# A fifth tile of rows by one-hot matmuls in 15 of 196 chunks, and moved zeros, of a graph-network kernel

## The chip, the cores and the metric

The kernel runs on one core of a Trainium2 chip. The metric is the time of one execution on the device in microseconds (us); lower is better. The core has a tensor engine (TensorE, PE in the profile, with its weight loads as PEld), a vector engine (DVE), a scalar engine (ACT), GpSimd (POOL) and a sync engine (SP). They run their own instruction streams and meet through semaphores. DMA transfers are issued by SP and ACT (queues "SPq" and "ACTq" in the profile) and by POOL, which issues the indirect ones.

## The reference

One layer of a graph network on 12,500 nodes with 32 features and 400,000 edges that are sorted by their target node:

```python
h = jnp.maximum(_layernorm(x, axis=-1), 0.0)
rol, col = (src, dst)
e_feat = jnp.concatenate([h[rol], h[col], edge_attr], axis=-1)
hid = jax.nn.relu(e_feat @ W1 + b1)                 # 96 -> 64
v = hid @ W2 + b2                                   # 64 -> 32
x_cand = jax.ops.segment_max(v, col, num_segments=num_nodes)
out = x + jnp.maximum(x_cand, h)
```

## The kernel before

**Tiling.** The nodes are padded to 12,544 = 128 x 98. The edges are cut into four stripes (NS = 4), which lie side by side on the 128 partitions, 32 features each. A chunk is 512 edges of each stripe, so 2,048 edges; there are 196 chunks. The main loop (from L530) takes two chunks c and c + 1 in an iteration, 98 iterations in all, and prepares chunks a = c + 2 and b = c + 3 for the next.

**Source rows.** For the 2,048 edges of a chunk the rows h[src] are wanted, 16 groups ("tiles") of 128. They come in two ways:

- Twelve by gathers: `gather(c)` (L148) issues twelve indirect DMAs on POOL, one for 128 rows of `h_d` in device memory. Three gathers share a buffer `gh`, and there are 24 buffers, so POOL can run ahead of their use by six chunks and then waits until DVE has read a buffer.
- Four by matmuls (MM = 4), in all chunks but the last: `tile(c, m)` (L227). The table h stands in `hs` as two parts, grouped by 7 (A1) groups of 14 (A0) nodes per partition. A key says which partition and group a source node lies in. `one_hots` (L202, DVE, five of the seven groups) and `one_hots_act` (L210, ACT, the other two) compare the keys with each partition's number and give `hot`. Seven times two matmuls of 448 columns in `tile` pick out, for each edge, the 14 nodes of its group; DVE multiplies them by a mask (`one`, L242) and reduces them (`gm`, L243) to the row. The products lie in two rotating PSUM buffers `pv`, which also hold the result of the second layer.

`to_features` (L245) transposes the rows to features on partitions, into `ht`: three gathered tiles at a time (L256), then the four from the matmuls (L259). L256 is what frees a `gh` buffer.

**Layers.** PE sums three products for each stripe into `ph`: edge attributes (`edges_into`), windows of the target nodes' part (`windows_into`) and `ht` (L548). ACT applies relu (`hid`, L552). PE multiplies by W2 (L569). DVE runs a segmented maximum along the edges (`sm`, L576). `leave_1` transposes it back (L473) and adds the bias (L475); `leave_2` selects the last edge of each node (L483, L487) and stores windows of 32 nodes into one of two tables, `top_d` (L491).

**Order.** Under `manual_schedule` the order of SP, PE, DVE and ACT is as written. In an iteration PE has tile(a, 0), the `ht` products of chunk c, tile(a, 1), tile(a, 2), the edge products of a, the W2 products, the window products of a, `leave_2` of the chunk before, tile(a, 3), `leave_1(c)`, tile(b, 0), `leave_2(c)`, tile(b, 1), `leave_1(c + 1)`, tile(b, 2) and tile(b, 3). POOL has little but gathers.

**Ahead of the loop.** h is computed in four pieces (three on DVE, one summed on POOL, squares on ACT, L327), stored to `h_d` (L337), and the gathers start. Keys are computed (L176 to L178) and stored to `key_d`, then read back repeated over the partitions (`load_keys`, L187). Just ahead of the loop ACT issues two DMAs that fill both tables `top_d` with zeros (L523), because not every node gets a store.

**Behind the loop.** A flag `general_i` says whether the input breaks the assumption that 512 edges of a stripe reach fewer than 32 nodes; it is computed by DVE and PE inside iteration 182 (L603 to L611). All engines load it and branch (L621, L622); with this input the general path is not taken. Then SP reads `top_d[0]` (L698) and ACT `top_d[1]` (L699), and DVE takes the maximum of both (L702), of that and h (L703), adds x (L704), and SP stores the output (L705), in four pieces.

Of the kernel before, what the change touches and what calls it, by code (L numbers as in the profile page):

```python
# [8 lines left out]
F32 = mybir.dt.float32  # L9
F32R = mybir.dt.float32r  # L10
F16 = mybir.dt.float16
# [12 lines left out]
P = 128  # L24
N = 12500
E = 400000
D = 32
# [26 lines left out]
LOW = 1e30  # L54
BY_ACT = range(A1 - 2, A1)
# [5 lines left out]
def ap(t, offset, dims):  # L61
    return bass.AP(tensor=t.tensor, offset=t.offset + offset, ap=dims)
# [3 lines left out]
def gnn_kernel(ctx, tc, x, src, src_mm, src_t, dst, dst_ext, lo, lo_c, ends_b, edge_attr, weights, w1, w2, b2, out):  # L66
# [28 lines left out]
    key_d = dram.tile([len(MMC) * MM * P], F16, name="key_d")  # L95
# [25 lines left out]
    for s in range(NS):  # L121
# [5 lines left out]
                   allow_small_or_imprecise_dtypes=True)  # L127
    hs = const.tile([P, 2, A1, D, A0], F32R, name="hs")
# [18 lines left out]

    def gather(c):  # L148
        n = min(K - MM * (c in MMC), (SE - c * C) // D)
        parts = []  # L150
        for k in range(0, n, SOME):
            parts.append(gathered.tile([P, SOME, D], F32, name="gh"))
            for i in range(min(SOME, n - k)):
                nc.gpsimd.indirect_dma_start(  # L154
                    out=parts[-1][:, i, :], out_offset=None, in_=h_d[:, :],
                    in_offset=bass.IndirectOffsetOnAxis(ap=src_i[:, c, k + i:k + i + 1], axis=0))
        return parts
# [13 lines left out]
    hts = {}  # L171
    loaded_b, ats = {}, {}
# [7 lines left out]
    def places(start, stop):  # L180

        se = src_i[:, MMC.start + start:MMC.start + stop, K - MM:]
        pk = place_k.rearrange("p (c m) -> p c m", m=MM)[:, start:stop]
        group(pk, se)
        nc.vector.scalar_tensor_tensor(pk, pk, -float(A0), se, op0=ALU.mult, op1=ALU.add)
# [41 lines left out]
    def tile(c, m):  # L227

        if c not in MMC:
            return  # L230
        if m == 0:
            mm_rows[c] = early.tile([P, MM, D], F32, name="gm", bufs=6)
        hot = hots[c]
        e = slice(m * P, (m + 1) * P)
        po = early_ps.tile([P, C], F32, name="pv", bufs=2)[:, :D * A0]
        for k in range(A1):
            for part in range(2):
                nc.tensor.matmul(po, hot[:, k, e], hs[:, part, k].rearrange("p f a -> p (f a)"),  # L238
                                 start=(k == 0 and part == 0), stop=(k == A1 - 1 and part == 1))
        of_group = po.rearrange("p (f a) -> p f a", a=A0)  # L240
        one = early.tile([P, D, A0], F32, name="one", bufs=2)
        nc.vector.tensor_tensor(one, of_group, masks[c][:, m, None, :].to_broadcast([P, D, A0]), op=ALU.mult)  # L242
        nc.vector.tensor_reduce(mm_rows[c][:, m, :], one, axis=AX.X, op=ALU.max)  # L243

    def to_features(c, part):  # L245

        if c >= NCH:
            return
        if c not in hts:
            hts[c] = early.tile([P, K, D], F32, name="ht", bufs=4)  # L250
        ht = hts[c]
        n = min(K - MM * (c in MMC), (SE - c * C) // D)
        if part < J:
            r = slice(part * SOME, min((part + 1) * SOME, n))
            if r.start < n:
                nc.vector.transpose(ht[:, r].rearrange("p k e -> p (k e)"),  # L256
                                    gh[c][part][:, :r.stop - r.start].rearrange("p k f -> p (k f)"))
        elif c in MMC:
            nc.vector.transpose(ht[:, n:].rearrange("p k e -> p (k e)"),  # L259
                                mm_rows.pop(c).rearrange("p k f -> p (k f)"))  # L260
        elif n < K:
            nc.vector.memset(ht[:, n:], 0.0)
# [26 lines left out]
    with tc.tile_pool(name="nodes", bufs=1) as pool, tc.tile_pool(name="nodes_ps", bufs=2, space=PSUM) as ps:  # L289
        sp = pool.tile([P, len(MMC) * MM], I32, name="sp")  # L290
        nc.scalar.dma_start(sp, src_mm)
        load_block(0, nc.sync)
        zero = early.tile([P, ZERO], F32, name="zero", bufs=1)
# [23 lines left out]
        for k in (0, 1, GP, 2):  # L317
            v, st, r = shares[k]
            n = r.stop - r.start
            total(v, st[:, 0, :n], xs[:, r])  # L320
            mean = st[:, 0, :n, None].to_broadcast([P, n, D])
            if v is nc.vector:
                v.scalar_tensor_tensor(h[:, r], mean, -1.0 / D, xs[:, r], op0=ALU.mult, op1=ALU.add)
            else:
                v.tensor_scalar(st[:, 0, :n], st[:, 0, :n], 1.0 / D, None, op0=ALU.mult)
                v.tensor_tensor(h[:, r], xs[:, r], mean, op=ALU.subtract)
            nc.scalar.activation(sq[:, r], h[:, r], AF.Square)  # L327
        for v, st, r in shares:
            n = r.stop - r.start
            total(v, st[:, 1, :n], sq[:, r])  # L330
            nc.scalar.activation(st[:, 0, :n], st[:, 1, :n], AF.Sqrt, scale=1.0 / D, bias=eps)
# [54 lines left out]
        key = pool.tile([P, len(MMC) * MM], F32, name="key")  # L386
        key16 = pool.tile([P, len(MMC) * MM], F16, name="key16")
# [40 lines left out]
    with tc.tile_pool(name="edges", bufs=3) as pool, tc.tile_pool(name="edges_ps", bufs=1, space=PSUM) as ps:  # L428
# [93 lines left out]
        for t in top_d:  # L522
            nc.scalar.dma_start(ap(t, 0, [[NT * D, P], [ZERO, NT * D // ZERO], [1, ZERO]]),  # L523
                                zero[:, None, :].to_broadcast([P, NT * D // ZERO, ZERO]))
# [5 lines left out]
        for c in range(0, NCH, 2):  # L530
# [10 lines left out]
            if a == NCH - 2:  # L541
                nc.gpsimd.tensor_tensor(again.rearrange("p (g a) f -> p g a f", a=A0),
                                        hs[:, 0].rearrange("p g f a -> p g a f"),
                                        hs[:, 1].rearrange("p g f a -> p g a f"), op=ALU.add)
            tile(a, 0)
# [27 lines left out]
            for x in range(2):  # L573
# [3 lines left out]
                sms.append(sm)  # L577
            tile(a, 3)
            one_hots_act(a + 2)
            to_features(a, 3)  # L580
            to_features(a, J)
# [20 lines left out]
            if c == (NB - 1) * BLOCK:  # L602
                nc.vector.tensor_scalar(bad[:, :NB, 1], bad[:, :NB, 1], float(W), None, op0=ALU.is_ge)  # L603

                nc.vector.tensor_tensor(bad[0:1, NB], lo_i[:, NCH - 1, :2], lo_i[:, 0, 2:], op=ALU.subtract)
                nc.vector.tensor_scalar(bad[0:1, NB], bad[0:1, NB], float(-W), None, op0=ALU.is_gt)
                worst = pool.tile([P, 1], F32, name="worst", bufs=1)
                nc.vector.tensor_reduce(worst, bad, axis=AX.XY, op=ALU.max)
                bp = ps.tile([P, J, P], F32, name="tr")[0:1, 0, 0:1]
                nc.tensor.matmul(bp, worst, ones, start=True, stop=True)  # L610
                nc.vector.tensor_copy(general_i, bp)  # L611
            leave = lambda c=c + 1, so=so, last=last[1]: leave_2(c, so, last)
        leave()


    with tc.tile_pool(name="out", bufs=1) as pool:
        acc = pool.tile([P, NT, D], F32, name="acc")
        part = pool.tile([P, NT, D], F32, name="part")

        top_v = [t.rearrange("(p t) f -> p t f", p=P) for t in top_d]  # L620
        flag = nc.values_load(general_i[0:1, 0:1], min_val=0, max_val=P)  # L621
        with tc.If(flag > 0):  # L622
            with tc.tile_pool(name="general", bufs=1) as gp, tc.tile_pool(name="general_ps", bufs=1, space=PSUM) as ps:
# [69 lines left out]
                nc.vector.memset(part, 0.0)  # L693
                for t, of in zip(top_v, (acc, part)):
                    nc.sync.dma_start(t, of)

        for r in pieces:
            nc.sync.dma_start(acc[:, r], top_v[0][:, r])  # L698
            nc.scalar.dma_start(part[:, r], top_v[1][:, r])  # L699
        out_v = out.rearrange("(p t) f -> p t f", p=P)  # L700
        for r in pieces:
            nc.vector.tensor_tensor(acc[:, r], acc[:, r], part[:, r], op=ALU.max)  # L702
# [66 lines left out]
```

## Time and profile before

| what | us | from |
|---|---|---|
| three runs, median (lowest, highest) | 4136.3 (4134.02, 4138.83) | the runs' times |
| the profiled execution, as given with the runs | 4138.83 | the runs' times |
| its span, first to last instruction | 4137.1 | the profile's page |
| first gather starts | 23.44 | timeline |
| first "hid" of the loop starts | 163.14 | timeline |
| first "hid" of iterations 186, 188, 190 and 192 | 3979.1, 4020.07, 4049.56, 4079.00 | timeline |
| last gather starts | 4014.42 | timeline |
| first read of `top_d` on ACT, on SP | 4113.93, 4115.77 | timeline |
| first maximum of the output, last addition ends | 4122.23, 4134.0 | timeline |

The mean granted TensorE clock of the execution was 0.892.

How to read the profile: a group or timeline row has engine, line, operation, "out<-in" by the program's names, shapes and count ("x14" is fourteen instructions merged into a row). "Idle before" is how long the engine had done nothing ahead of an instruction, with what ended it; "issue" stands for a wait that the profile explains by nothing, "remote" for a semaphore whose setter it does not name. PE's matmuls are pipelined: a row of fourteen lasts less than fourteen times the mean of one. "PEclk" or "clock" is the share of full TensorE clock that was granted, and the DMA share is the mean busy share of the core's 16 DMA engines.

The DMA engines in the first microseconds, from busy time by stage:

| stage, us | 8:10 | 10:12 | 12:14 | 14:16 | 16:18 | 18:20 | 20:22 | 22:24 | 70:75 | 75:80 | 80:85 | 85:90 |
|---|---|---|---|---|---|---|---|---|---|---|---|---|
| DMA share | 0.99 | 0.97 | 0.48 | 0.00 | 0.22 | 0.91 | 0.88 | 0.05 | 0.23 | 1.03 | 0.76 | 0.32 |
| GB/s | 419 | 387 | 165 | 0 | 86 | 362 | 341 | 17 | 64 | 393 | 260 | 67 |

### The profile page before, as it was taken

How to read it: one execution, taken by the hardware profiler on the slowest of the kernel's cores; microseconds unless marked ns; L12 is line 12 of the kernel's file. 1: busy time of each engine (PE TensorE's matmuls, PEld its weight loads, DVE VectorE, ACT ScalarE, POOL GpSimd, SP SyncE). 2: the span in 40 equal slices, each digit the busy share in tenths (PEclk: the TensorE clock that was granted, in tenths of full speed). 3: DMA queues.
4: the chain of work that ended last, by engine and by line, in shares of the span. 5: the costliest groups of instructions: out<-in, count | busy, mean ns of one | idle time of the engine just before them, and what ended most of it. 6: DMA issues, size and time to landing. Idle time of an engine off the chain costs nothing. (4 is left out here: it accounts for less than half of the span.)

```text
span 4137.1 us, 58828 instructions
## 1 busy us (share of the span) xinstructions
PE 3622.7 (88%) x21189; PEld 2423.9 (59%) x21189; DVE 2238.2 (54%) x3869; ACT 1117.3 (27%) x1795; POOL 2258.4 (55%) x2376
## 2 busy tenths in 40 slices
PE   3588888998999998899899999998898889999986
PEld 3456565656566665656565656565656565555664
DVE  4355555555555555555555555555555555555565
ACT  3132223222222222222222232323232323222232
POOL 6555555555555555555555555555555555555550
PEclk7799999989888889999998989898999998988898
DMA  5123222322232222222222222232223222322221
GB/s 196 35 43 64 52 48 43 69 51 44 48 64 53 44 47 65 51 43 52 65 46 46 58 57 49 43 65 53 46 45 66 52 47 46 65 52 44 47 66 51
DMA packets 194678, 229.58 MB, mean 55 GB/s; under 512 B 118333, under 2 KB 158797, under 8 KB 181582
## 3 DMA queue, kind: packets, MB, share of 16 engines
q10 hardware_dynamic: 32580, 110.55, 9.5%
q1 hardware_dynamic: 86762, 76.67, 8.1%
q0 software_dynamic: 75040, 38.57, 7.3%
q8 instruction: 167, 2.74, 0.3%
q14 instruction: 129, 1.06, 0.1%
HBM read 211.68 MB, written 13.85 MB: 55 GB/s over the span
## 5 line engine op out<-in xcount | busy, mean ns | idle before, releaser
L154 POOL DMA_INDIRECT gh<-h_d,src_i x2345 | 2237.3, 954 | 1763.7 <-DVE ht L256 662.3
L238 PE MATMUL pv<-hs,hot 128*128 128x448 f32 x10920 | 2432.0, 373 | 261.3 <-DVE one L242 112.5
L238 PEld LDWEIGHTS pv<-hs,hot 128*128 128x128 f32 x10920 | 2014.1, 190 | 596.2 <-issue 208.3
L242 DVE TENSOR_TENSOR one<-pv,mask 128x448 f32<-128x448 f32 x780 | 480.0, 615 | 1740.3 <-PE pv L238 832.3
L552 ACT ACTIVATE hid<-ph,wt 128x512 f32<-128x512 f32 x392 | 266.2, 688 | 1945.9 <-PE ph L497 632.1
L207 DVE TENSOR_TENSOR hot<-kb,consts 128x1536 fp32r<-128x1536 f16 (+2 forms) x388 | 565.9, 1458 | 0.0
L243 DVE TENSOR_REDUCE gm<-one 128x32 f32<-128x448 f32 x780 | 483.7, 620 | 26.9
L497 PE MATMUL ph<-ea,wt 32*64 32x512 f32 x1568 | 381.8, 781 | 122.3 <-issue 103.1
L569 PE MATMUL pv<-hid,wt 64*32 64x512 f32 x1568 | 341.2, 1008 | 56.8 <-DVE one L242 51.2
L217 ACT ACTIVATE hot<-away,ones 128x512 fp32r<-128x512 f32 x392 | 283.4, 723 | 93.1 <-ACT away L216 52.1
L576 DVE TENSOR_TENSOR_SCAN sm<-pb,sm,pv 128x512 f32<-128x512 bf16 x195 | 249.5, 1280 | 93.5 <-PE pv L569 71.1
L487 ACT ACTIVATE wo<-tr 128x64 f32<-128x64 f32 x196 | 43.8, 223 | 908.0 <-remote 634.4
L216 ACT ACTIVATE away<-kb,key_n 128x512 f32<-128x512 f16 x392 | 277.9, 709 | 0.0
L497 PEld LDWEIGHTS ph<-ea,wt 32*64 32x64 f32 x1568 | 83.2, 149 | 327.6 <-issue 287.0
L483 PEld LDWEIGHTS tr<-so,last 128*64 128x64 f32 x3136 | 126.0, 157 | 184.9 <-issue 155.2
L569 PEld LDWEIGHTS pv<-hid,wt 64*32 64x32 f32 x1568 | 37.3, 133 | 319.1 <-DVE one L242 222.5
L256 DVE STREAM_TRANSPOSE ht<-gh 128x96 f32<-128x96 f32 x782 | 209.8, 268 | 0.0
L497 PE MATMUL ph<-of,qw 32*64 32x512 f32 x1568 | 189.6, 1027 | 0.9 <-issue 0.8
L483 PE MATMUL tr<-so,last 128*64 128x64 f32 x3136 | 155.6, 249 | 8.0 <-issue 4.1
L459 ACT ACTIVATE of<-db,below 128x512 f32<-128x512 int32 x196 | 139.0, 709 | 18.4 <-DMA db<-in_dst_ext 18.4
L460 ACT ACTIVATE of<-of,ones 128x512 f32<-128x512 f32 x196 | 141.5, 722 | 6.4
L497 PE MATMUL ph<-ht,wt 32*64 32x512 f32 x1568 | 126.2, 618 | 8.7 <-DVE ht L259 5.5
(77 smaller groups left out, 783.9 us busy)
## 6 DMA issues: line engine op xcount, KB each, us to landing
ea<-in_edge_attr SPq DMA_DIRECT2D x49, 1024.0 KB
db<-in_dst_ext ACTq DMA_DIRECT2D x48, 1024.0 KB
gh<-h_d,src_i POOLq DMA_INDIRECT x2345
pb<-pen_d ACTq DMA_DIRECT2D x48, 512.0 KB
kb<-key_d ACTq DMA_DIRECT2D x95, 256.0 KB
qw<-q_d SPq DMA_DIRECT2D x784, 8.0 KB
top_d<-wo SPq DMA_DIRECT2D x784, 4.0 KB
top_d<-zero ACTq DMA_DIRECT2D x2, 1568.0 KB
```

The costliest lines, as they stand in the source:

```text
L154: nc.gpsimd.indirect_dma_start(out=parts[-1][:, i, :], out_offset=None, in_=h_d[:, :], in_offset=bass.IndirectOffsetOnAxis(ap=src_i[:, c, ...
L207: nc.vector.tensor_tensor(hot_of(c)[:, start:stop], keys[c][:, None, :].to_broadcast([P, n, MM * P]), key_ps[:, start:stop, None].to_broad ...
L216: nc.scalar.activation(away, keys[c], AF.Square, bias=key_n[:, k:k + 1])
L217: nc.scalar.activation(hot_of(c)[:, k], away, AF.Relu, bias=ones, scale=-1.0)
L238: nc.tensor.matmul(po, hot[:, k, e], hs[:, part, k].rearrange("p f a -> p (f a)"), start=(k == 0 and part == 0), stop=(k == A1 - 1 and par ...
L242: nc.vector.tensor_tensor(one, of_group, masks[c][:, m, None, :].to_broadcast([P, D, A0]), op=ALU.mult)
L243: nc.vector.tensor_reduce(mm_rows[c][:, m, :], one, axis=AX.X, op=ALU.max)
L483: nc.tensor.matmul(pw[g * 2 * W:(g + 1) * 2 * W], last[:, j, 2 * g:2 * g + 2].rearrange("p s w -> p (s w)"), so[:, j, g * 2 * D:(g + 1) * ...
L497: nc.tensor.matmul(ph[s][x * HID:(x + 1) * HID], w[g], e[g], start=start, stop=stop)
L552: nc.scalar.activation(hid[s], ph[s], AF.Relu, bias=b1c)
L569: nc.tensor.matmul(pv[x][s * D:(s + 1) * D], w2x[g], hid[s][g], start=True, stop=True)
L576: nc.vector.tensor_tensor_scan(sm, loaded.pop(c + x)[2], pv[x], before, op0=ALU.add, op1=ALU.max)
```

## The change

1. In chunks 6, 18, 30, ... 174 (MORE, 15 chunks, always an `a` of the loop) only eleven tiles are gathered. The twelfth comes by `tile_more`: a key load of 32 KB on ACT's queue (`load_more`), a one-hot over all seven groups and a mask on DVE (`hot_more`), fourteen matmuls, multiplication, reduction (`pick`, which `tile` now uses too) and a transpose of its own. The one-hots, mask and row have buffers of their own.
2. The zeros of `top_d` are issued in front, on ACT's queue behind the first two squares, instead of just ahead of the loop. Their source buffer goes to the pool that ends with that stage.
3. The flag is computed behind the loop instead of in iteration 182.
4. The tables are read and their maximum is taken ahead of the branch, and the general path overwrites `acc` instead of rewriting the tables.

```diff
+MORE = range(6, NCH - 12, 12)
...
+    def gathers(c):
+        return min(K - MM * (c in MMC) - (c in MORE), (SE - c * C) // D)
+
     def gather(c):
-        n = min(K - MM * (c in MMC), (SE - c * C) // D)
+        n = gathers(c)
...
+        more = src_i[:, MORE.start:MORE.stop:MORE.step, K - MM - 1]
+        for pk, se in ((place_k.rearrange("p (c m) -> p c m", m=MM)[:, start:stop],
+                        src_i[:, MMC.start + start:MMC.start + stop, K - MM:]),
+                       (place_m, more))[:1 + (start == 0)]:
+            group(pk, se)
+            nc.vector.scalar_tensor_tensor(pk, pk, -float(A0), se, op0=ALU.mult, op1=ALU.add)
...
+    def load_more(c):
+        if c in MORE:
+            kb = early.tile([P, P], F16, name="kb_more", bufs=1)
+            nc.scalar.dma_start(kb, ap(key_d, (len(MMC) * MM + MORE.index(c)) * P, [[0, P], [1, P]]))
+            keys_more[c] = kb
+
+    def hot_more(c):
+        if c in MORE:
+            hot = early.tile([P, A1, P], F32R, name="hot_more", bufs=1)
+            nc.vector.tensor_tensor(hot, keys_more[c][:, None, :].to_broadcast([P, A1, P]),
+                                    key_ps[:, :, None].to_broadcast([P, A1, P]), op=ALU.is_equal)
+            mask = early.tile([P, A0], F32, name="mask_more", bufs=1)
+            k = MORE.index(c)
+            nc.vector.tensor_tensor(mask, place_ps, place_m[:, k:k + 1].to_broadcast([P, A0]), op=ALU.is_equal)
+            keys_more[c] = hot, mask
+
+    def tile_more(c):
+
+        if c in MORE:
+            rows = early.tile([P, D], F32, name="gm_more", bufs=1)
+            pick(*keys_more.pop(c), rows)
+            nc.vector.transpose(hts[c][:, K - MM - 1], rows)
...
+            if k < len(top_d):
+                nc.scalar.dma_start(ap(top_d[k], 0, [[NT * D, P], [ZERO, NT * D // ZERO], [1, ZERO]]),
+                                    zero[:, None, :].to_broadcast([P, NT * D // ZERO, ZERO]))
...
-        for t in top_d:
-            nc.scalar.dma_start(ap(t, 0, [[NT * D, P], [ZERO, NT * D // ZERO], [1, ZERO]]),
-                                zero[:, None, :].to_broadcast([P, NT * D // ZERO, ZERO]))
...
+            load_more(a)
             tile(a, 0)
...
+            hot_more(a)
             tile(a, 3)
             one_hots_act(a + 2)
             to_features(a, 3)
+            tile_more(a)
             to_features(a, J)
...
-            if c == (NB - 1) * BLOCK:
-                nc.vector.tensor_scalar(bad[:, :NB, 1], bad[:, :NB, 1], float(W), None, op0=ALU.is_ge)
...
         leave()
+        nc.vector.tensor_scalar(bad[:, :NB, 1], bad[:, :NB, 1], float(W), None, op0=ALU.is_ge)
...
+        for r in pieces:
+            nc.sync.dma_start(acc[:, r], top_v[0][:, r])
+            nc.scalar.dma_start(part[:, r], top_v[1][:, r])
+        for r in pieces:
+            nc.vector.tensor_tensor(acc[:, r], acc[:, r], part[:, r], op=ALU.max)
         flag = nc.values_load(general_i[0:1, 0:1], min_val=0, max_val=P)
...
-                nc.vector.memset(part, 0.0)
-                for t, of in zip(top_v, (acc, part)):
-                    nc.sync.dma_start(t, of)
-        for r in pieces:
-            nc.sync.dma_start(acc[:, r], top_v[0][:, r])
-            nc.scalar.dma_start(part[:, r], top_v[1][:, r])
...
         for r in pieces:
-            nc.vector.tensor_tensor(acc[:, r], acc[:, r], part[:, r], op=ALU.max)
             nc.vector.tensor_tensor(acc[:, r], acc[:, r], again[:, r], op=ALU.max)
```

## The prediction

> **What bounds the kernel now.** I read the page first: the engines' totals and the 40 slices.
>
> ```profile
> PE 3622.7 (88%) x21189; PEld 2423.9 (59%) x21189; DVE 2238.2 (54%) x3869; ACT 1117.3 (27%) x1795; POOL 2258.4 (55%) x2376
> ...
> PE   3588888998999998899899999998898889999986
> ...
> POOL 6555555555555555555555555555555555555550
> PEclk7799999989888889999998989898999998988898
> ```
>
> TensorE (PE) is busy for 88%, evenly over the loop, and GpSimd (POOL) for 55%. POOL's last slice is empty: the gathers end before the matmuls. That end is a natural experiment, so I asked for busy time by stage: the loop with gathers (93 iterations, from the first of the four "hid" activations at 163.10 to the one at 3979.10), and two iterations behind the last gather.
>
> ```profile
> 163.10:3979.10 3816.00, 3442.03 (x20078) 2291.68 (x20077) 2091.95 (x3636) 1039.63 (x1673) 2121.74 (x2229) 0.90 0.25 52
> ...
> 4020.10:4049.60 29.50, 29.50 (x217) 23.63 (x218) 22.20 (x39) 10.92 (x19) 11.95 (x1) 1.00 0.21 58
> 4049.60:4079.00 29.40, 29.40 (x217) 23.58 (x217) 22.15 (x39) 10.85 (x19) 0.00 (x0) 1.00 0.01 2
> ```
>
> The columns are length, then busy time and count of PE, its weight loads, DVE, ACT and POOL, the granted clock, DMA share, GB/s. With gathers an iteration takes 3816.0/93 = 41.03 us; without, 29.4 to 29.5 for the same eight matmul tiles, with PE busy all the time at clock 1.00. So the matmul work is 29.45 us, and 24 gathers beside it cost 11.6 us, though no engine but POOL runs them (POOL's 11.95 in the first of the two windows is one addition, L542, that waits for the last gather). The groups show what they are, and the timeline of one iteration how they cost.
>
> ```profile
> L154 POOL DMA_INDIRECT gh<-h_d,src_i x2345 | 2237.3, 954 | 1763.7 <-DVE ht L256 662.3
> L238 PE MATMUL pv<-hs,hot 128*128 128x448 f32 x10920 | 2432.0, 373 | 261.3 <-DVE one L242 112.5
> ```
>
> ```profile
> 2009.91 1.11 PE L497 MATMUL ph<-ht,wt 32*64 32x512 f32 x16
> ...
> 2012.10 0.69 ACT L552 ACTIVATE hid<-ph,wt 128x512 f32<-128x512 f32 x1 [15.14 <-PE ph L497]
> ...
> 2014.25 0.69 ACT L552 ACTIVATE hid<-ph,wt 128x512 f32<-128x512 f32 x1 [1.47 <-PE pv L238]
> ...
> 2017.05 0.69 ACT L552 ACTIVATE hid<-ph,wt 128x512 f32<-128x512 f32 x1 [2.11 <-remote]
> ...
> 2018.04 0.95 POOL L154 DMA_INDIRECT gh<-h_d,src_i  x1 [0.30 <-issue]
> ...
> 2020.56 0.69 ACT L552 ACTIVATE hid<-ph,wt 128x512 f32<-128x512 f32 x1 [2.82 <-remote]
> ...
> 2021.37 0.62 DVE L242 TENSOR_TENSOR one<-pv,mask 128x448 f32<-128x448 f32 x1 [8.78 <-remote]
> ```
>
> All sixteen matmuls that the four activations wait for end by 2011.02. Behind the last gather the four start 0.6 us apart (one merged row of 2.43 us); here they start 2.15, 2.80 and 3.51 us apart, and DVE gets a product that PE ended near 2014 only at 2021.37. In this time POOL issues twelve gathers without a pause, the last at 2018.04; when it stops, all goes on. So long runs of gathers hold up the handing over from PE to ACT and DVE. POOL itself has room: 24 x (0.95 + 0.30) = 30 us of 41, the rest spent waiting for DVE to free its buffers. PE's work is on the path; of a gather, only this hold-up is.
>
> The start shows the same, larger: POOL's first gather is at 23.44, released by the store of h_d; it runs until it has no free buffer, and DVE's waits of 13.48, 34.62 and 36.64 us lie in that run.
>
> ```profile
> 136.52 0.95 POOL L154 DMA_INDIRECT gh<-h_d,src_i  x1 [0.30 <-issue]
> ...
> 140.53 0.62 DVE L242 TENSOR_TENSOR one<-pv,mask 128x448 f32<-128x448 f32 x1 [36.64 <-remote]
> ```
>
> **The change, part by part.** Sums are against the profiled execution's span, 4137.1 us. That run is given as 4138.83, 2.5 above the median 4136.3, so I add the difference to the median.
>
> *The tile, PE.* 15 chunks (6, 18, ... 174) get 14 matmuls more, put right behind tile(a, 3) and ahead of the transposes of leave_1. Fourteen of L238 take 3.07 us (timeline at 2003.18, x14); at half clock 5.38 (at 102.00, x14, in a stretch with clock 0.50). Behind the insertion stand leave_1, tile(b, 0..3) and the next "hid", all on PE's path. In the stretch PE is idle (3816.0 - 3442.0)/93 = 4.0 us per iteration, 10%; I let the tile fill its share of that, 0.3. So +2.76 each. Bounds: 0, all in idle time, and 5.38.
>
> *The gather.* 15 of 2345 go. Average price: (41.03 - 29.45)/24 = 0.48 us. Bounds: 0, since POOL has room, and 1.25, its whole place in a run. I take 0.48, the only price measured with the hold-up in it. Net 2.28 x 15 = +34.2; with the outer bounds -19 to +81.
>
> The Trainium skill ("TensorE: Matmul & The Clock Gate", Part 1) says that about 3.4 us of PE idleness halves the clock and as much activity restores it. The slices and the 0.90 of the loop against 1.00 behind it agree that the gathers' waits cost clock. If the tile filled such a hole it would earn 3.4 us of full clock, some 1.7 us of work, an estimate from that page; the sum would then be 15 x 0.6 = +9 instead of +34. No row here shows a hole of this kind filled, so the sum stays.
>
> *DVE and ACT for the tile.* hot_more is 896 elements: between the 1024-element form of L207 (1.18 us) and zero, about 1.03 by proportion; mask at most 0.20 (L222); one 0.62, reduce 0.62, transposes at most 0.27. 2.7 us on an engine with 2092/3816 = 55% load. hot_more stands behind the two scans, where DVE idles 3.33 us before its next "one" (2033.27), so it is hidden there; without that cover it delays PE by up to 1.2 us, 18 in all. Queued behind one_more is leave_1's addition, whose PE input is itself later by the tile. The 32 KB key load is one issue on ACT's queue (0.33 us, as kb at 2037.90) ahead of a 15 us wait for "hid"; hidden. Nothing is added.
>
> *Zeros.* Two stores of 1568 KB move from 73.40 to ACT's queue behind the first two squares (8.11 and about 11.2). The issue costs ACT 0.6 us each (L523); the first lies in ACT's idle 2.18 us, the second delays the square that POOL's sum waits for: 0.5. The data go behind that queue's loads, which the 2 us windows show moving until about 13. In 75 to 85 us the zeros showed 393 and 260 GB/s, 8.3 us for both. The DMA engines are free from 14 to 16 (share 0.00) and mostly to 18 (0.22), then 0.91 and 0.88 with h_d's stores: some 5.5 us fit, 2.5 push h_d back. POOL's run starts with h_d and ends the stage, so +3 passes on. The old place was under POOL's run, at cadence 1.25 all through, so nothing is gained there. Bounds: 0, and 6, had they no room at all; a whole wait of DVE (36.6) more or less is possible, since I can't say what ends the first two, and lies in the tails.
>
> The skill's "DMA: Bandwidth & Descriptors", section "Issuing engines are not separate DMA queues", speaks against this move: whatever engine starts them, transfers run on the same 16 engines and interleave. By it alone, all 3.2 MB beside h_d, it would be the upper bound, 6.
>
> *The end.* The reads of top_d no longer wait for the branch on SP: SP's first stood at 4115.77 (L698), ACT's at 4113.93 (L699), so -1.8. DVE meets its own branch between the maxima and the sums, where it was idle before: load 0.48 and compare 0.4 by PE's rows there, about +0.9; it can no longer overlap later pieces' loading, so up to +1 more. The flag's six small DVE operations (at most 0.4 each) now run in DVE's 15.18 us wait. Together -0.5, from -3 to +2. The shorter general path isn't taken and costs nothing. place_m's four small operations (0.2 to 0.37, as L176 to L185) add up to 0.9 near 38 us, ahead of pen: +0.3.
>
> Sum: 34.2 + 3 - 0.5 + 0.3 = **+37, 4173 us**.
>
> **Rivals.** (1) *Absorbed.* The tile lies in PE's 4.0 us of idle time, the gather earns 0.48: 15 x (-0.48) + 3 = -4, 4132; with a third of the tile on the path, 4147. For: the idle time is larger than the tile. Against: it is scattered in waits for PE's own products, behind which the tile comes, and "sm", "so" and the next tiles come after it. (2) *Faster: the shorter run.* The run of gathers sets the iteration: each gather gone ends a hold-up 1.25 us earlier while the tile goes on in idle time: 15 x (-1.25) = -19, with the rest 4121. It decides once the tile costs PE under 1.25 us of path. For: the four "hid" starts end with the run. Against: POOL waits for DVE 11 us an iteration, so its runs are set by what DVE frees, and without gathers the iteration is PE's alone. (3) *Half clock.* The tile falls into the slow part, 5.38 - 0.48 = 4.9, x 15 = +73, 4213 with the start. For: about a fifth of the time is at half clock (mean 0.90). Against: only this fifth. (4) That the change does nothing of what it says is out: by instruction order PE gets 15 groups of 14, POOL 2330 gathers.
>
> **Chances.** Forecast (4150 to 4200) 0.56, absorbed 0.16, faster 0.20, half clock or worse 0.08. What can be told from no change is 0.2%, 8.3 us. Above 4144.6: the forecast, rival 3 and a fifth of the absorbed, 0.67; within: 0.12, the rest of the absorbed but its lowest part; faster: 0.21. The range from 4124 to 4202 leaves out about 0.1 below (most of rival 2 lies near or under its 4121) and 0.1 above; the forecast's own is 4150 to 4200.
>
> **What would show it.** Right: iterations with a fifth tile some 2 to 3 us over their neighbours, about 41.0 elsewhere; fourteen matmuls of L269 on hot_more in about 3.1 us; first gather near 26; reads of top_d on SP near 4114 plus the shift. Wrong: equal iterations and less PE idle time (rival 1); shorter ones (rival 2); hot_more matmuls of 0.4 us spacing (rival 3); a start stage that moved by tens of us, which would hide the loop's share.

## The result, and the profile after

The changed kernel takes 4159.67 us (median of 22 runs, 4142.69 to 4177.34) against 4136.18 (22 runs) for the kernel before: ratio 1.0054, interval 1.0043 to 1.0065, so +23.5 us: slower, by half a percent. The profiled execution of the changed kernel is one of its shorter ones (4154.5, span 4152.7), so its trace shows 15.6 us of the 23.5. Three rows of its page, to be read beside those of before:

```profile
PE 3632.4 (87%) x21399; PEld 2481.6 (60%) x21399; DVE 2279.8 (55%) x3948; ACT 1107.8 (27%) x1795; POOL 2240.6 (54%) x2361
...
L159 POOL DMA_INDIRECT gh<-h_d,src_i x2330 | 2220.0, 953 | 1794.5 <-DVE ht L287 666.6
L269 PE MATMUL pv<-hs,hot 128*128 128x448 f32 x10920 | 2468.9, 378 | 207.4 <-issue 92.9
```

PE has 210 matmuls more, 9.7 us more busy time in all and a share of 87 instead of 88%. 210 matmuls at 0.2 us are 42 us: most of them were paid for elsewhere. Busy time by stage shows where (columns as in the prediction): the loop, one iteration with a fifth tile between two without, and one behind the last gather.

```profile
167.81:3993.52 3825.71, 3448.24 (x20284) 2347.94 (x20285) 2131.10 (x3704) 1030.35 (x1673) 2108.07 (x2215) 0.91 0.25 52
1937.14:1979.62 42.48, 39.52 (x224) 26.12 (x223) 23.51 (x41) 11.21 (x18) 23.86 (x26) 0.88 0.26 52
1979.62:2023.80 44.18, 39.99 (x225) 26.42 (x223) 23.37 (x43) 11.21 (x19) 22.89 (x25) 0.88 0.19 46
2023.80:2065.41 41.61, 38.02 (x218) 26.68 (x218) 22.21 (x39) 10.87 (x18) 21.71 (x23) 0.88 0.28 48
4034.44:4064.18 29.74, 29.74 (x217) 23.55 (x217) 22.20 (x39) 10.90 (x19) 11.94 (x1) 1.00 0.15 47
```

The loop's 93 iterations take 3825.71, 9.7 more than the 3816.00 of before. From the starts of "hid" in both traces: the 15 iterations with a fifth tile take 45.18 on average (the same 15 in before 41.35, so +3.83, +57 in all), the other 78 take 40.36 (before 40.97, so -0.61, -48 in all). The tile costs more where it stands than it brings, and gives most of it back in the iterations around it.

The tile itself runs as forecast, at full clock. A row of the timeline, with what stands ahead of it on DVE and its product's use behind it:

```profile
1996.83 1.06 DVE L251 TENSOR_TENSOR hot_more<-kb_more,consts 128x896 fp32r<-128x896 f16 x1
...
2000.11 3.00 PE L269 MATMUL pv<-hs,hot_more 128*128 128x448 f32 x14
...
2003.14 0.62 DVE L273 TENSOR_TENSOR one<-pv,mask_more 128x448 f32<-128x448 f32 x1 [1.41 <-PE pv L269]
```

The fourteen take 3.00 us, and each of the 210 matmuls in the 15 places lasts 360 to 369 ns, so none fell into half clock. Next the start, where the zeros moved; one row is an issue on ACT's or SP's queue or an instruction of POOL:

```profile
7.34 0.63 ACTq L360 DMA_DIRECT2D top_d<-zero  x1
...
11.81 0.56 ACTq L360 DMA_DIRECT2D top_d<-zero  x1
...
16.98 3.86 SPq L371 DMA_DIRECT2D h_d<-h  x4
...
27.86 1.18 POOL L159 DMA_INDIRECT gh<-h_d,src_i  x1 [12.65 <-DMA h_d<-h]
```

The same two steps in the kernel before:

```profile
16.75 3.86 SPq L337 DMA_DIRECT2D h_d<-h  x4
...
23.44 1.18 POOL L154 DMA_INDIRECT gh<-h_d,src_i  x1 [9.07 <-DMA h_d<-h]
```

The stores of h_d are issued 0.23 us later than before, but the first gather starts at 27.86 instead of 23.44: by busy time by stage the DMA engines have a share of 0.91 to 1.05 from 12 to 24 us, where before they were free from 14 to 16. The first "hid" of the loop is at 167.81 instead of 163.14, so the 4.4 us of the first gather arrive there as 4.7. And the end:

```profile
4129.59 2.04 SPq L654 DMA_DIRECT2D acc<-top_d  x4
4129.61 2.08 ACTq L655 DMA_DIRECT2D part<-top_d  x4
4134.68 1.09 DVE L657 TENSOR_TENSOR acc<-acc,part 128x896 f32<-128x896 f32 x1 [8.63 <-DMA part<-top_d]
```

The last "wo" is at 4125.40, and SP's first read of a table comes 4.2 us behind it (before: 4108.09 and 4115.77, 7.7). From the last "wo" to the end it is 27.3 us instead of 29.0. Between the loop's 93 iterations and that end stand four more, three of them behind the last gather: they take 120.4 us instead of 118.6. So the 15.6 us of the trace are 4.7 at the start, 9.7 in the loop, 1.8 in these four and -0.5 from the last iteration's first "hid" to the end.

### The profile page after: what moved, and what is told of

Same layout as the page of the kernel before. It is cut to its first block, busy times and chain, and to the rows that moved or that the text cites. A ratio compares the mean times of both kernels' runs of the same rounds, so it can differ in the third digit from the quotient of the medians.

```text
span 4152.7 us, 59320 instructions
## 1 busy us (share of the span) xinstructions
PE 3632.4 (87%) x21399; PEld 2481.6 (60%) x21399; DVE 2279.8 (55%) x3948; ACT 1107.8 (27%) x1795; POOL 2240.6 (54%) x2361
## 5 line engine op out<-in xcount | busy, mean ns | idle before, releaser
L269 PE MATMUL pv<-hs,hot 128*128 128x448 f32 x10920 | 2468.9, 378 | 207.4 <-issue 92.9
L269 PEld LDWEIGHTS pv<-hs,hot 128*128 128x128 f32 x10920 | 2045.6, 192 | 553.2 <-issue 202.2
L584 ACT ACTIVATE hid<-ph,wt 128x512 f32<-128x512 f32 x392 | 256.8, 688 | 1706.1 <-PE ph L531 765.4
L601 PE MATMUL pv<-hid,wt 64*32 64x512 f32 x1568 | 313.1, 946 | 124.3 <-DVE one L273 88.0
L531 PE MATMUL ph<-ea,wt 32*64 32x512 f32 x1568 | 308.1, 707 | 73.2 <-issue 56.6
L287 DVE STREAM_TRANSPOSE ht<-gh 128x96 f32<-128x96 f32 (+1 forms) x782 | 209.4, 268 | 0.0
L531 PEld LDWEIGHTS ph<-ea,wt 32*64 32x64 f32 x1568 | 64.8, 141 | 240.2 <-issue 221.1
L531 PE MATMUL ph<-ht,wt 32*64 32x512 f32 x1568 | 146.4, 648 | 46.2 <-DVE ht L290 44.7
```

The costliest lines, as they stand in the source:

```text
L269: nc.tensor.matmul(po, hot[:, k], hs[:, part, k].rearrange("p f a -> p (f a)"), start=(k == 0 and part == 0), stop=(k == A1 - 1 and part = ...
L531: nc.tensor.matmul(ph[s][x * HID:(x + 1) * HID], w[g], e[g], start=start, stop=stop)
L584: nc.scalar.activation(hid[s], ph[s], AF.Relu, bias=b1c)
L601: nc.tensor.matmul(pv[x][s * D:(s + 1) * D], w2x[g], hid[s][g], start=True, stop=True)
```

## The experiments

Twelve kernels ran, in four comparisons, each against the kernel before on the same chip at the same time. They fell under two conditions, without which the numbers can't be read: the kernel before took 4213 us in the first comparison (as in the result, 4136, its products are handed over late) and 3050, 3049 and 3048 in the other three (nothing is handed over late, an iteration takes 30.3 us). Some expectations speak of two kinds of chip; that was wrong, since the first and the last comparison ran on the same chip. What sets the condition stayed open. Only ratios within a comparison are used; the absolute times in the expectations were reckoned from 4136, and are read as differences.

**First comparison, before = 4212.98: the parts of the change, and its loop part six times as often.**

No fifth tile; the zeros, the flag and the reads stay moved:

```diff
-        return min(K - MM * (c in MMC) - (c in MORE), (SE - c * C) // D)
+        return min(K - MM * (c in MMC) - (c in USE), (SE - c * C) // D)
...
+USE = ()
```

> The changed kernel with no fifth tile in any chunk (16 tiles as before: twelve gathers, four by matmuls); the moved zeros, the later flag and the earlier reads of the tables stay. My account: the zeros in front of h_d's stores cost about +4.2 us of start (first gather near 27.9 instead of 23.4), the end gives -1.6, so +2 to +4 on before, 4138 to 4140, with about 41.0 us per iteration as in before. Rival 'the moves are the cost': most of the +23 is here, 4152 to 4160. Rival 'the start shift is absorbed': at or below before, 4131 to 4136, although the first gather is late.

Measured: 4220.59, ratio 1.0015 (1.0006 to 1.0024), +6.3 us; first gather at 27.77. Somewhat more than my +2 to +4, whose upper end lies inside the interval. So the moves are about a quarter of the change's 0.54%, and the fifth tiles are the rest: (0.0054 - 0.0015) x 4136 = 16 us (10 to 22 by the two intervals), 1.1 each.

The fifth tile in every even chunk from 6 to 182:

```diff
-MORE = range(6, NCH - 12, 12)
+MORE = range(6, NCH - 12, 2)
```

> The fifth tile in every even chunk from 6 to 182 (89 instead of 15), so six times as often. My account: net of a fifth tile is (23 - 2.8)/15 = 1.35 us, 89 of them +120, with the moved zeros and the end 4255 to 4265; by the forecast's 2.28 each it would be 4342. Rival 'a tile gives back most of itself in the iterations around it' (the profiled execution of the changed kernel, loop +11.5 for 15, 0.77 each): 4190 to 4210. Rival 'the clock recovers': the granted clock rises from 0.897 to over 0.92.

Measured: 4354.47, ratio 1.0307 (1.0268 to 1.0346), +129. Less the +6.3 this is 1.38 per tile, as my account had it.

The same, and the twelfth gather is done too:

```diff
+MORE = range(6, NCH - 12, 2)
...
-        return min(K - MM * (c in MMC) - (c in MORE), (SE - c * C) // D)
+        return min(K - MM * (c in MMC), (SE - c * C) // D)
```

> As the kernel with 89 fifth tiles, but the twelfth gather of these chunks is done as well (its row is then overwritten by the same row from the matmuls): the price of a tile alone. My account: 3.07 less a tenth of idle time, 2.8 each, 89 of them +246, so about 4385; the difference to the kernel that drops the gather is then the price of a gather, 0.5 to 1.4 each (43 to 125 in all). Rival 'the tile lies in idle time': under +1.3 each, below 4255, and no more than 20 us from the kernel that drops the gather.

Measured: 4355.07, ratio 1.0342 (1.0322 to 1.0363), +144. The tile alone costs (0.0342 - 0.0015) x 4213 / 89 = 1.55, not 2.8; and beside the tile the gather is worth 0.17, which its interval can't tell from nothing. My account missed; so did the rival's 1.3, though the closeness to the kernel without the gather is the rival's.

The twelfth gather left out, with nothing in its place (its row is set to zero):

```diff
+MORE = range(6, NCH - 12, 2)
...
-            pick(*keys_more.pop(c), rows)
-            nc.vector.transpose(hts[c][:, K - MM - 1], rows)
+            nc.vector.memset(hts[c][:, K - MM - 1], 0.0)
...
-            load_more(a)
...
-            hot_more(a)
```

> In the same 89 chunks the twelfth gather is left out and nothing takes its place: its row is set to zero, so one sixteenth of the source rows of these chunks is not computed. No fifth tile, keys, one-hot or mask. The price of a gather alone. By the mean price 0.48: 89 x 0.48 = 43 less, plus 2.8 for the moves, 4096. By its whole place in a run, 1.25: -111, 4028. Rival 'POOL has room, a gather is free': 4135 to 4140. If prices add up, this and the tile alone sum to the kernel with 89 fifth tiles.

Measured: 4080.36, ratio 0.9698 (0.9671 to 0.9726), -127. Without the moves a gather alone is worth 1.50, more than its whole place of 1.25. Tile +1.55 and gather -1.50 would sum to 0.05; together they are +1.38. The prices do not add up, so both must pay for, or save, the same thing. Stages of an iteration, in us, means over the 89 iterations from p = 2 to 90 of each trace (p counts the iterations from 0), from the first "hid" by way of the second scan and the two additions of `leave_1` (L475 in before) to the next first "hid":

| kernel | hid to 2nd scan | to 1st addition | to 2nd addition | to next hid | iteration |
|---|---|---|---|---|---|
| before (in its own comparison) | 16.69 | 6.17 | 9.96 | 8.25 | 41.07 |
| no fifth tile | 17.07 | 6.26 | 10.22 | 8.31 | 41.86 |
| 89 fifth tiles | 16.34 | 9.21 | 6.71 | 11.19 | 43.45 |
| 89, gather kept | 16.52 | 9.20 | 6.72 | 10.87 | 43.31 |
| 89 gathers less, no tile | 16.33 | 6.20 | 6.90 | 10.74 | 40.17 |

The tile costs its full 2.95 in the stage where it stands. In the next stage all three kernels save 3.3 to 3.5, whether a tile was added or a gather dropped, and the last stage takes 2.4 to 2.9 of it back. The 3.4 is the same wait in nearly every iteration. In the timeline of the kernel without a fifth tile it looks like this:

```profile
2284.89 0.95 POOL L160 DMA_INDIRECT gh<-h_d,src_i  x1 [4.96 <-DVE ht L291]
...
2286.97 3.11 PE L270 MATMUL pv<-hs,hot 128*128 128x448 f32 x14
...
2289.92 0.60 PE L508 MATMUL tr<-ident,sm 128*128 128x128 f32 x4
...
2291.19 0.95 POOL L160 DMA_INDIRECT gh<-h_d,src_i  x1 [0.30 <-issue]
2293.57 0.62 DVE L274 TENSOR_TENSOR one<-pv,mask 128x448 f32<-128x448 f32 x1 [4.53 <-PE pv L270]
```

And in the kernel with 89 tiles and the gather kept, at the same place of its iteration:

```profile
2347.62 3.13 PE L269 MATMUL pv<-hs,hot 128*128 128x448 f32 x14
...
2348.85 0.95 POOL L159 DMA_INDIRECT gh<-h_d,src_i  x1 [2.67 <-DVE ht L287]
...
2350.59 0.60 PE L507 MATMUL tr<-ident,sm 128*128 128x128 f32 x4
2350.79 0.62 DVE L273 TENSOR_TENSOR one<-pv,mask 128x448 f32<-128x448 f32 x1 [1.10 <-issue]
```

In the first, a tile's product ends near 2290.1 and PE goes on to the transposes, but DVE gets it at 2293.57; POOL has by then issued six gathers in a row, from 2284.89 to 2291.19. In the second, POOL had paused 2.67 us ahead of 2348.85, and DVE takes the product at once. The tile puts more time between the two transposes on DVE that free these gathers' buffers; the dropped gather leaves a buffer with two gathers instead of three, so POOL is through before the next buffer comes free. Either cuts the run of six, and it can be cut only once.

The last stage shows where the hold-up goes. From p = 2 to 89 the product of tile(b, 2) reached DVE over 0.5 us late in 2 of 88 iterations without a fifth tile, in 55 with the 89 tiles, in 60 with the gather kept and in 65 with the gathers dropped; for tile(b, 3) it was 0, 36, 30 and 25. Cut at tile(b, 1), the run stands behind the later products instead, and of the 3.3 to 3.5 us only 0.6 to 0.9 stay won by the table's last two stages.

The trace of the changed kernel, with its 15 tiles, shows both effects apart. Stage "to 2nd addition" of its first 24 iterations, L over 9 us, s under 8, ? anything else:

```
after, p = 0 to 23:   LLsLLsLLsLLsLLs??sLLsLLs
before, p = 0 to 23:  LLLLLLLL?LLLLLLLLLsLLLLL
```

Fifth tiles stand at p = 2, 8, 14, 20. There the tile cuts the run. At p = 5, 11, 17, 23 there is no tile, but there POOL, which by its 24 buffers is three iterations ahead, issues the eleven gathers of the next such chunk. In the kernel without the gather, s ends at p = 87, three iterations before its last such chunk at p = 90; in the one that keeps the gather, s runs from p = 2 to 90.

So in the changed kernel the two cuts stand in different iterations, and the one wait that both remove is shown for the 89 tiles alone. With 15 the prices of either alone, +1.55 and -1.50, would come to 0.05 each; measured was 1.1 (0.7 to 1.5 by the two intervals). In its trace, against the same iterations of before, those with a fifth tile take 3.83 us more, those at p = 5, 11, 17 ... 1.82 less (-27 of the -48), those one later 1.17 less (-18). Single iterations differ by up to 9 us either way, so this split is rough. Why a tile's net is 1.1 there, and not nothing, stayed open.

Counted over the tiles' products in the trace of before, by how many gathers POOL had issued without a pause (starts under 1.4 us apart) when the product ended, and how many reached DVE over 0.5 us late, counted from when both the product and DVE were ready:

| gathers in a row | before: products | late | mean late, us | five traces of the other condition: products | late |
|---|---|---|---|---|---|
| 0 to 3 | 393 | 4 | 0.8 | 212 | 0 |
| 4 | 4 | 1 | 7.3 | 27 | 0 |
| 5 | 166 | 108 | 3.2 | 53 | 0 |
| 6 to 9 | 95 | 81 | 7.0 | 220 | 0 |
| 10 and more | 46 | 0 | | 3053 | 0 |

(The 46 end with the last gathers of a run of twelve; that the end of a run ends the wait is my reading of it.) So it goes by runs, not by a price per gather: with up to three in a row nearly every product is in time, with six to nine most are late. With four it can't be said: in the five other traces of this condition 12 of 25 were late.

But the rows of this table are also different products. The 166 with five in a row are above all those of tile(a, 0), late in 15 of 73, and of tile(b, 1), late in 85 of 85. So five in a row are not enough by themselves. Free of this is the same product with and without the run: that of tile(b, 1) was late with five in a row in 85 of 85 iterations of before, 86 of 86 without a fifth tile and 58 of 58 of the changed kernel; with at most three it was late in 1 of 30 of the changed kernel and in none of 88 in either kernel with 89 tiles. In before it has at most three in a row in three iterations, with no tile or gather touched (p = 18, 36 and 71): there it waits 0.6, 1.3 and 0.7 us instead of 3.3. That the iteration gets shorter by it is not shown: the one at p = 18 takes 44.5 us.

**Second comparison, before = 3049.99.** It was meant to test this by cutting runs alone. The transpose that frees b's first buffer moved back:

```diff
-            to_features(b, 0)
             one_hots(a + 2, 0, 2)
+            to_features(b, 0)
```

> The kernel before with one line of DVE's order changed: the transpose that frees the gather buffer of b's first part comes behind the one-hot of 1.18 us that followed it. No tile, gather or matmul is added or removed. Theory 'runs of gathers': a product's handing over from PE to DVE is late only when POOL has issued more than about four gathers in a row; here the run of six behind a's last part is cut into 3 + 3, so the time from the first to the second addition of the second layer's result falls from 10.2 to about 6.8 us in nearly every iteration, and the time by about 90 us (60 to 140; ratio 0.966 to 0.986). Rival 'the gather itself costs' (its transfers, its share of memory): nothing changes, ratio 0.998 to 1.002; or slower by up to 1.2 us an iteration.

A pause on POOL behind each third gather, POOL's order as written:

```diff
+            nc.gpsimd.memset(pause, 0.0)
```

> The kernel before with a pause on POOL: behind each third gather POOL writes 128 x 128 zeros to a buffer that nobody reads, and POOL's order is as written too. Same gathers, same tiles. Theory 'runs of gathers': no run is longer than three, so the late handing over (10.2 us an iteration summed over the products of tiles, counted in the traces) goes; POOL needs 24 x 1.257 + 8 x 0.3 = 33 us an iteration, PE 29.5, so an iteration takes 33 to 38 us, ratio 0.82 to 0.93. Rival 'only an idle POOL ends a run': POOL is as busy as in a run, nothing falls, ratio 1.00 to 1.01. Rival 'the gather itself costs': 1.00 to 1.02.

The change with this pause:

> The changed kernel (15 fifth tiles, moved zeros and end) with the same pause behind each third gather. Theory: without held-up products a tile has nothing to pay it back and costs its 3.0 us of PE: 15 x 3.0 + 4 to 6 for the moves, about +50 on the kernel before with pauses. If POOL then sets the iteration (33 us against PE's 29.5), the tile is free instead and only +4 to +6 or less remain. Rival 'a pause changes nothing': +20 to +25 as without it.

The change with the zeros issued from ACT's queue where the keys are stored in the program:

```diff
-            if k < len(top_d):
-                nc.scalar.dma_start(ap(top_d[k], 0, [[NT * D, P], [ZERO, NT * D // ZERO], [1, ZERO]]),
...
         load_keys(0, nc.sync)
+        for k in range(len(top_d)):
+            nc.scalar.dma_start(ap(top_d[k], 0, [[NT * D, P], [ZERO, NT * D // ZERO], [1, ZERO]]),
```

> The changed kernel with the zeros of the tables issued behind the stores of h_d, on the same queue, a few us later than in the change. My account: the late first gather (27.9) comes of the zeros moving ahead of h_d's stores, so it is back near 23.7 and the time falls by about 4 us against the changed kernel (ratio to before 1.0035 to 1.005 instead of 1.0054). Rival 'the zeros compete with the first gathers and keys wherever they are': first gather near 23.7, and the first activation of the loop as late as in the change (167.8), no gain.

Measured: 3050.11, ratio 1.0004 (0.9994 to 1.0013); 3106.14, 1.0185 (1.0169 to 1.0200); 3169.38, 1.0383 (1.0364 to 1.0402); 3180.19, 1.0438 (1.0423 to 1.0453). With nothing late there was nothing to cut, so the first two can't tell the theories apart. They tell something else: POOL's cadence sets the iteration here. With the pause three gathers take 3.86 us by the timeline, eight times 30.9, and the iteration 30.94; without, 24 x 1.257 = 30.2 against 30.3, while PE alone needs 29.5. In the last kernel the zeros were behind h_d by their issue and not by their transfer: ACT issued them at 18.08 and 18.76, 1.4 us after h_d's first store, and the first gather came at 28.85, later still, so this miss too was mine.

The change itself did not run under this condition. With later zeros it cost 4.4% here, and 1.9% with the pause on both sides (1.0383 against 1.0185; +63 us, near the expected 50, but for another reason than PE's 3.0 a tile). Iterations with a fifth tile took 39.9 and, with the pause, 40.3, the others 29.9 and 29.8. The view of the tile kb_more in the kernel with later zeros, and the two rows of one such iteration:

```profile
its engine sat idle before it (us, times) until:
  DMA kb_more<-key_d: 87.5, 15
```

```profile
1472.50 0.33 ACTq L245 DMA_DIRECT2D kb_more<-key_d  x1
...
1500.84 1.09 DVE L251 TENSOR_TENSOR hot_more<-kb_more,consts 128x896 fp32r<-128x896 f16 x1 [7.66 <-DMA kb_more<-key_d]
...
1502.07 5.57 PE L269 MATMUL pv<-hs,hot_more 128*128 128x448 f32 x14 [7.03 <-DVE mask_more L255]
```

The 32 KB of keys, issued at 1472.50 behind two loads of 1.0 and 0.5 MB, arrive 28 us later (24 to 28 in the 15 places); DVE waits 7.66 for them (87.5 in all 15), PE 7.03, and after this idleness the fourteen matmuls take 5.57 instead of 3.00, at a granted clock of 0.53 (1502 to 1508 us). In the other places they take 4.4 to 5.6. The Trainium skill ("TensorE: Matmul & The Clock Gate", Part 1) says that about 3.4 us without work halves the clock; this row agrees. In the changed kernel's own trace the load is issued at 1968.25 and used at 1996.83, 28.6 later, and DVE waited only 0.6 us in all, in 2 of the 15 places: the cover, 28.0 to 29.8, was there, with little to spare.

**Third comparison, before = 3049.09.**

```diff
-            load_more(a)
+            load_more(a + 2)
```

> The changed kernel with the key load of a fifth tile issued one iteration earlier; in the change it stands on ACT's queue behind two loads of 1.0 and 0.5 MB of the same iteration. Two kinds of chip have shown up, so both are stated. Where the kernel before takes 3050 us (no held-up products, iteration 29.5 to 30.3): the fifth tile's one-hot waited 87.5 us in all for this load; without it, and without the tile at half clock behind the wait (5.57 instead of 3.0), 15 x (5.8 + 2.5) = 125 us go from the +133, ratio 1.000 to 1.010 instead of 1.044. Where the kernel before takes 4130 to 4220: the one-hot waited 0.6 us in all, so nothing changes, ratio 1.003 to 1.007. Rival 'the tile itself is the cost': on both kinds no change from the earlier placing.

```diff
+            for _ in range(3):
+                nc.gpsimd.memset(pause, 0.0)
```

> The kernel before with three writes of 128 x 128 zeros on POOL behind each third gather, so that POOL pauses by some 0.6 us (one such write had stretched the gap by 0.1 only). Where the kernel before takes 4130 to 4220, theory 'runs of gathers hold up products': no product of a tile waits any more, an iteration takes 35 to 38 us instead of 41 to 42, ratio 0.83 to 0.93; rival 'a pause is no remedy, only fewer gathers': 1.00 to 1.02. Where the kernel before takes 3050: nothing is held up anyway and POOL becomes the bound, 24 x 1.257 + 8 x 0.6 = 35 us an iteration against 30.3, ratio 1.12 to 1.17.

The moved transpose, once more:

> The kernel before with the transpose that frees b's first gather buffer behind the one-hot of 1.18 us, once more, for a chip on which the kernel before takes 4130 to 4220. Theory 'runs of gathers': the run of six is cut into 3 + 3, the time from the first to the second addition of the second layer's result falls from 10.2 to about 6.8 us, the whole by 60 to 140 us, ratio 0.966 to 0.986. Rival 'the gather itself costs': 0.998 to 1.002. On a chip with 3050 us: no change, as measured.

Measured: 3058.35, ratio 1.0028 (1.0017 to 1.0040); 3787.7, 1.2422 (1.2398 to 1.2447); 3050.57, 1.0007 (0.9997 to 1.0017). The keys an iteration earlier take nearly all of the 4% away, inside the expected range (the kernel with the 4.4% also had the zeros elsewhere, which moved its first "hid" by 2 us); the tile then starts without a wait and at full clock:

```profile
1439.27 1.06 DVE L251 TENSOR_TENSOR hot_more<-kb_more,consts 128x896 fp32r<-128x896 f16 x1
...
1441.06 2.99 PE L269 MATMUL pv<-hs,hot_more 128*128 128x448 f32 x14
```

Its iterations take 32.56, the others 29.87: here, where PE has no idle time, the tile costs 2.7. The gather nearly pays it back, since POOL's 30.2 was the longer of the two: all iterations together take 30.30 on average, and 30.23 in the kernel with the moved transpose. The long pause was mis-sized, as POOL's rows show:

```profile
999.06 0.96 POOL L155 DMA_INDIRECT gh<-h_d,src_i  x1 [0.50 <-DVE last L468]
...
1002.53 0.74 POOL L159 MEMSET pause<- 128x128 f32 x3
1003.77 0.96 POOL L155 DMA_INDIRECT gh<-h_d,src_i  x1 [0.49 <-DVE one L245]
```

Three writes and the gap around them make 4.71 per three gathers, and 8 x 4.71 = 37.7 is the iteration of 38.0. It fits a POOL bound, not my 35. The moved transpose met the same condition again, so cutting a run without touching tile or gather remains untested where runs matter.

**Fourth comparison, before = 3047.76.** In the traces of the changed kernel and all made from it, a tile's matmuls (the second to the last of the fourteen, tiles under 215 ns) start 203.9 to 204.2 ns apart on average, medians 204.3 to 204.4, in those from the kernel before 201.2 to 201.8, median 200.4. With the keys ahead, place_m was moved so that hs starts where it did:

```diff
-    place_m = const.tile([P, len(MORE)], F32, name="place_m")
     hs = const.tile([P, 2, A1, D, A0], F32R, name="hs")
     place_k = const.tile([P, len(MMC) * MM], F32, name="place_k")
+    place_m = const.tile([P, len(MORE)], F32, name="place_m")
```

> The changed kernel with the keys an iteration earlier, and with place_m allocated behind hs and place_k instead of ahead of hs: the table hs then starts at the address it has in the kernel before (64 bytes lower than in the change), all else stays where the change has it. In the traces of all kernels made from the one before, a tile's matmuls start 200.1 ns apart at full clock, in all made from the change 204, on every chip. Theory 'the table's address': the spacing is 200 again, 112 x 0.0038 = 0.4 us less in each iteration. Where the kernel before takes 3050, PE sets the iteration: 98 x 0.35 = -34 on the 1.0028 of the kernel with keys ahead, ratio 0.990 to 0.994, below both kernels. Where it takes 4130 to 4220, part of it lies in idle time: ratio 0.998 to 1.004, from 1.0054. Rival 'the new way of slicing, or the other buffers, slow the matmuls': spacing stays 204, ratio 1.0015 to 1.004 (or 1.0054).

Measured: 3059.16, ratio 1.0038 (1.0024 to 1.0052), no better than without it. The spacing fell to 203.5 on average (median 201.8), part of the way, while that of the fifth tile's own matmuls rose from 202.1 to 204.1; an iteration without gathers stayed at 29.73 (before: 29.45). The theory falls for the time. What makes a gather-free iteration of the changed kernel 0.28 us longer is open. No version that computes the whole result beat the kernel before.

## Why the prediction was right, and where its steps were not

The forecast of 4173 was right in sign and kind, and the measured 4159.67 lies in the forecast's own range; its size was +37 against +23.5.

- *What bounds the kernel.* PE on the path, POOL with room, and runs of gathers that hold up the handing over to DVE and ACT: the traces agree. What was not in the text: a run of up to three gathers holds up almost nothing, the same product behind five waits, and a run cut at one product holds up a later one. Taking an average of 0.48 per gather out of an effect that goes by runs was the step that had the worst size.
- *The tile, +2.76.* The matmuls took the 3.00 (forecast 3.07), at full clock, and all of it showed in the stage where they stand (+2.95). But the price alone was 1.55 an iteration (89 tiles). I had 10% of idle time pay for it; in fact a wait of 3.5 us in the next stage went away, and 2.6 of it came back in the stage behind.
- *The gather, -0.48, bounds 0 and 1.25.* Alone 1.50, outside the bounds; beside the tile 0.17. "Net 2.28" summed two prices that are not independent where tile and dropped gather meet the same run, as with the 89; measured together it is 1.38 for 89 and 1.1 for 15, where they don't meet and the difference to the sum of both prices stays open.
- *Zeros, +3 (0 to 6).* First gather +4.4, first "hid" +4.7, inside the bounds, by the mechanism named: transfers in front of h_d's. No wait of 36 us came or went.
- *The end, -0.5 (-3 to +2).* From the first "hid" of the last iteration to the end 38.76 instead of 39.30, so -0.5; from the last "wo" -1.7. The moves measured +6.3 (2.5 to 10.1) against +2.8 forecast with place_m's 0.3; start and end make 4.1 of it by the changed kernel's trace. The sum has nothing for the four iterations behind the loop's 93, which that trace shows 1.8 longer.
- *DVE and ACT at nothing.* It held in this comparison, for a reason I had not checked: I priced the key load's issue (0.33) and not its 24 to 28 us to landing. Where an iteration is 30 us, the wait for the same load was most of a loss of 4%.
- *Rivals.* "Half clock" did not occur under this condition. "Absorbed" and "shorter run" each hold a part: the other iterations did get shorter, by 0.61, and a gather less did end a hold-up, by cutting a run rather than by 1.25 each.
- *What would show it.* Iterations with a fifth tile were to be 2 to 3 us over their neighbours with the rest unchanged; they were 4.8 over, with the rest 0.61 shorter. The sum came out near for that reason, not because each term was right. By the prices of either alone, 1.55 and 1.50, the loop would have cost nothing; that the sum still came inside the range is partly luck. Reads of top_d "near 4114 plus the shift" were at 4129.6.

## What to carry to other kernels

Before two prices are summed, ask whether both act on the same wait: here, done in every iteration, a tile added or a gather dropped removed the same wait of 3.4 us, and only kernels with one, the other and both showed it. Then ask where a wait goes that is removed: most of this one came back a stage later. An average over a stage with and without something (11.6 us for 24 gathers) is not the price of one more or one less where the effect goes by the length of runs. A transfer hidden today needs its landing time beside its cover, not its issue time: 24 to 28 us under a cover of 28 to 30 is no cover once the loop runs faster.

## What was not expected of the hardware

- Under one condition products of PE reached DVE late when POOL had issued five or more gathers without a pause (before: 189 of 261 with five to nine in a row, 4 of 393 with up to three), though not each product alike; under the other, with runs of hundreds, none of 3565 was late, and the same kernel took 3048 to 3050 instead of 4136 to 4213. The chip with the 4213 later gave 3048, so it is not the chip alone; what it is was not found.
- Two things that looked like the code's belong to the same condition: the granted clock of 0.89 (0.99 in the other, for the kernel before) and the 163 us to the loop's first activation (85 and 88 in the two runs with the moved transpose).
- Matmuls of one shape start 200.4 or 204.4 ns apart (medians) depending on the build, whatever the chip; with the moving table 64 bytes lower it was 201.8, and for the fifth tile's 2 ns more.
